# Four small edits in the gated layers: up products copied by ScalarE, squares on GpSimd, down products started from half of the features, two pieces more at the heads' norm

## The chip, the cores and the metric

The kernel runs on one core of a Trainium2 chip. A core has five engines that run their own instruction queues side by side: TensorE (PE, matrix products, with weight loads as PEld), VectorE (DVE), ScalarE (ACT), GpSimd (POOL), and SyncE (SP), which here issues DMAs. They share an on-chip memory (SBUF); PE writes its products into eight accumulator banks (PSUM), which DVE and ACT read. The metric is the device time of one launch in microseconds (us). All data is float32.

## The reference

Eight sequences of 512 tokens with 256 channels go through four residual layers, each `x = x + layer(...)`:

```python
x = x + attention(layernorm(x))       # 16 heads of 16 channels, 60% of the queries kept
x = x + routed_ffn(layernorm(x))
x = x + gated_layer(layernorm(x))     # linear attention over 8 steps, then swiglu, inside its own residuals
x = x + routed_ffn(layernorm(x))      # the same weights again
```

The change touches the last three. The routed layer picks 4 of 16 blocks of 64 hidden features for each token and computes `relu(x @ w1.T + b1)`, masked to the picked blocks, times `w2.T`. The gated layer:

```python
q, k, v, alpha, out_gate = ...        # projections of rmsnorm(x); alpha from a small gate net
S = alpha * S + k (outer) v;  o = q . S                # 16 heads of 16 channels, step by step
o = (o - mean(o)) / sqrt(var(o) + 1e-5)                # per head and token: "the heads' norm"
x = x + (o * out_gate) @ wo.T
x = x + (silu(n @ w_gate.T) * (n @ w_up.T)) @ w_down.T   # n = rmsnorm(x), 1024 features: "swiglu"
```

The eight sequences are the eight steps of the linear attention, so a slice of 128 positions can be worked through all layers alone.

## The kernel before, in words

The first 600 us are the attention of the first layer, with the scores of all heads. It is not touched. After it the tokens, which stay in SBUF as `xres` (128 positions x 8 sequences x 4 slices x 256 channels), are worked on in four slices `k` of 128 positions. For each slice there is an output projection of the attention, a routed layer, the linear attention `gla(k)`, `swiglu(k)` and a second routed layer.

Two kinds of work are woven into each other by `between(units, pieces, n)`: after each unit of a list it calls as many `next(pieces)` as keep `n` pieces spread evenly over the units. Units are the large matmuls; pieces are the stretches between two `yield`s of the generators `gla` and `route`, with most of DVE's, ACT's and POOL's work. The lists at the end of the program put, for example, the rest of `gla(2)` and the beginning of `gla(3)` beside `swiglu(1)`. The number of pieces of one `gla` is the constant `GLA`. The program's order is not the final one: a scheduler of the tile framework orders each engine's instructions again from its own estimates, and puts semaphore waits where data or buffers require it.

- **Units of a routed layer** (`routed_ffn`). For each half `g` of the sequences (512 columns) and each of 8 groups `f` of 128 hidden features: two matmuls 128x512 into a bank `h_ps` (L909), a ReLU with bias by ACT to SBUF (L917; in the last layer, every second by DVE, L915), and a multiplication by the mask on DVE (L918). Then the down product.
- **Units of swiglu**. For each `g` and `f` two units: gate, two matmuls into a bank `swi_ps` (L936) and a Silu by ACT into a tile `h` (L942); up, two matmuls into another bank and a product `h * up` on DVE, which reads the bank (L945). Then the down product.
- **The down product** (`down`, L880 to L899). For a pair `u` of sequences, two columns blocks `i` of one bank `y_ps`, each the sum over 8 features (L889, matmuls of 256 columns). A unit is four matmuls: half of the features of one block. When both blocks are full, DVE adds the bank to `xres` (L894). A half `g` has two pairs, so eight units.
- **Banks.** `h_ps` and `swi_ps` share three banks, `y_ps` has two, the pieces' products share three. Tiles `h` have eight buffers; other tiles of the pool `post` have two unless it is said.
- **Pieces of `gla`**: statistics, transposes into channels, projections (L1019) copied by ACT (L1024), then for each of two halves `m` of the heads a series of weighted sums: DVE computes products and sums (L1042, L1044, L1052) in a tile `pr`, POOL adds them up in `o` (L1069). `hold` (L876 to L878) makes POOL write one element of a tile that is about to be used from the newest swiglu or routed result, so that this series cannot run ahead of the units.
- **The heads' norm** ends the series of each `m`: `sq = o * o` by ACT (L1114), `o = o * gate` on POOL (L1115), the sum of the squares per head on DVE (L1116, `var`). After both `m`: square root by ACT (L1123), reciprocal on DVE (L1124), and `o = o * var` on DVE for each `m` (L1127). Then PE transposes `o` (L1136, `oT_ps`), ACT copies it (L1137) and the output projection `gla_y` follows (L1144).

Of the kernel before, what the change touches and what calls it, by code (L numbers as in the profile page):

```python
# [10 lines left out]
F32 = mybir.dt.float32  # L11
U8 = mybir.dt.uint8
AF = mybir.ActivationFunctionType
ALU = mybir.AluOpType
# [3 lines left out]
P = 128  # L18
NB = 8
L = 512  # L20
D = 256
# [17 lines left out]
def block_kernel(ctx: ExitStack, tc: tile.TileContext, t: dict, out: bass.AP):  # L39
    nc = tc.nc  # L40
# [58 lines left out]
    with ExitStack() as outer:  # L99
# [25 lines left out]
        with ExitStack() as inner:  # L125
# [413 lines left out]
            for n in range(len(steps) + LAG + 1):  # L539
# [47 lines left out]
                else:  # L587
                    if n >= LAG:
                        next(later, None)
                    b, i = divmod(n - LEAD, 16)  # L590
# [19 lines left out]
        w2 = load_chunked(wpool, "w2", t["f_w2T"], nc.sync)  # L610
        b2 = load_rows(wpool, "b2", t["L0_ffn_b2"], nc.sync)

        with tc.tile_pool(name="a_tail", bufs=2) as tail:
# [7 lines left out]
            for u in range(2):  # L621
                for m in range(NC2):
                    for i in range(4):
                        b = 2 * i + u
                        rows = bass.ts(i, 32)
                        ps = (bank if i % 2 else bank_m)(f"nrm_ps{b}")
# [42 lines left out]
    w_down = load_chunked(wpool, "w_down", t["b_w_downT"], nc.sync)  # L669
# [15 lines left out]
    post = ctx.enter_context(tc.tile_pool(name="post", bufs=2, side="right", reuse_waits="tile"))  # L685
    dram = ctx.enter_context(tc.tile_pool(name="dram", bufs=2, space=bass.MemoryType.DRAM))

    def bank_h(name):
        return ps_h.tile([P, 512], F32, tag="h", name=name)

    def bank_y(name):
        return ps_y.tile([P, 512], F32, tag="y", name=name)
# [7 lines left out]
    G4 = NB // 2  # L700
# [12 lines left out]
    def tokens(k, b, n=2):  # L713
        return xres[:, b : b + n, k, :]

    def pairs(y):
        return y.rearrange("p (b d) -> p b d", d=D)
# [159 lines left out]

        nc.gpsimd.tensor_copy(dst, newest[0])  # L878

    def down(h, w, k, g, u, last):  # L880

        b = G4 * g + 2 * u
        y = []

        def unit(i, half):
            if i == 0 and half == 0:
                y.append(bank_y("y_ps"))
            for f in range(NF // 2 * half, NF // 2 * (half + 1)):
                nc.tensor.matmul(  # L889
                    y[0][:, bass.ts(i, D)], h[f][:, bass.ts(2 * u + i, P)], w[:, f, :],  # L890
                    start=(f == 0), stop=(f == NF - 1),
                )
            if i == 1 and half == 1:
                nc.vector.tensor_tensor(tokens(k, b), tokens(k, b), pairs(y[0]), ALU.add)  # L894
                newest[0] = xres[0:1, b, k, 0:1]
                if last:
                    nc.sync.dma_start(out=out_v[:, b : b + 2, k, :], in_=tokens(k, b))

        return [functools.partial(unit, i, half) for i in range(2) for half in range(2)]  # L899

    def hidden():
        return post.tile([P, 512], F32, tag="h", name="h", bufs=8)
# [1 line left out]
    def routed_ffn(k, key, last):  # L904
        def unit(h, g, f):
            xT, mk = ready[key]
            ps = bank_h("h_ps")
            for c in range(NC2):
                nc.tensor.matmul(  # L909
                    ps, w1[:, c, bass.ts(f, P)], xT[g][:, c, :],  # L910
                    start=(c == 0), stop=(c == NC2 - 1),
                )
            hf = hidden()
            if last and f % 2:
                nc.vector.tensor_scalar(hf, ps, b1[:, f : f + 1], 0.0, ALU.add, ALU.max)  # L915
            else:
                nc.scalar.activation(hf, ps, AF.Relu, bias=b1[:, f : f + 1])  # L917
            nc.vector.tensor_tensor(hf, hf, mk[g][:, f, :], ALU.mult)  # L918
            h.append(hf)
            newest[0] = hf[0:1, 0:1]  # L920

        units = []
        for g in range(2):
            h = []
            units += [functools.partial(unit, h, g, f) for f in range(NF)]
            for u in range(2):
                units += down(h, w2, k, g, u, last)
        return units


    def swiglu(k):
        def unit(h, pg, g, f, w):
            zT = ready["z", k]
            ps = bank_h("swi_ps")
            for c in range(NC2):
                nc.tensor.matmul(  # L936
                    ps, w[:, c, bass.ts(f, P)], zT[g][:, c, :],
                    start=(c == 0), stop=(c == NC2 - 1),
                )
            if w is w_gate:  # L940
                hf = hidden()
                nc.scalar.activation(hf, ps, AF.Silu)  # L942
                h.append(hf)
            else:
                nc.vector.tensor_tensor(h[f], h[f], ps, ALU.mult)  # L945
                newest[0] = h[f][0:1, 0:1]

        units = []
        for g in range(2):
            h = []  # L950
            for f in range(NF):
                units += [functools.partial(unit, h, None, g, f, w) for w in (w_gate, w_up)]
            for u in range(2):
                units += down(h, w_down, k, g, u, False)
        return units


# [3 lines left out]
    def gla(k):  # L961
# [18 lines left out]
        ps = bank_l("gh_ps")  # L980
# [12 lines left out]
        for u in range(2):  # L993
            ps = [bank_l("al_ps") for g in range(2)]
# [6 lines left out]
            for g in range(2):  # L1001
                b = G4 * g + 2 * u
# [10 lines left out]
        o = [rest.tile([P, NB, P], F32, tag="o", name="o", bufs=2) for m in range(NC2)]  # L1013
# [48 lines left out]
        def heads(m):  # L1062


            def fours(x):
                return x.rearrange("p (u i) n -> p u i n", i=G4)

            def add(dst, src):
                nc.gpsimd.tensor_tensor(dst, dst, src, ALU.add)  # L1069

            made = rest.tile([P, 3, NB, P], F32, tag="made", name="made")
            gate = rest.tile([P, NB, P], F32, tag="gate", name="gate", bufs=2)
            for b in range(NB):
                project(made, gate, m, b)
                yield
            nc.scalar.activation(gate, gate, AF.Silu)
            key, q, v = (fours(made[:, i]) for i in range(3))
            a, out = fours(al[:, :, bass.ts(m, P)]), fours(o[m])

            def near(d):  # L1080
                n = G4 - d
                if d > 0:
                    nc.gpsimd.tensor_tensor(
                        key[:, :, 0:n, :], key[:, :, 0:n, :], a[:, :, d:, :], ALU.mult
                    )
                return q[:, :, d:, :], key[:, :, 0:n, :], v[:, :, 0:n, :]

            pr = weighed([near(0)])[0]
            nc.gpsimd.tensor_copy(out, pr)
            yield from pause(5)  # L1090
            pr = weighed([near(1)])[0]
            add(out[:, :, 1:, :], pr)
            yield from pause(4)
            for d in (2, 3):
                pr = weighed([near(d)])[0]
                add(out[:, :, d:, :], pr)
                yield from pause(4 - d // 3)
            nc.gpsimd.tensor_tensor(q[:, 1, 0, :], q[:, 1, 0, :], a[:, 1, 0, :], ALU.mult)
            nc.gpsimd.tensor_tensor(
                q[:, 1, 1:, :], q[:, 1, 1:, :], far[:, :, bass.ts(m, P)], ALU.mult  # L1100
            )
            every = [P, 2, G4, P]
            for s in (0, 2):
                pr = weighed([(
                    q[:, 1].unsqueeze(1).to_broadcast(every),
                    key[:, 0, s : s + 2, :].unsqueeze(2).to_broadcast(every),
                    v[:, 0, s : s + 2, :].unsqueeze(2).to_broadcast(every),
                )])[0]
                for i in range(2):
                    add(out[:, 1], pr[:, i])  # L1110
                yield from pause(5)
            sq = rest.tile([P, NB, P], F32, tag="pr", name="sq", bufs=2)
            hold(sq[0:1, 0, 0:1])
            nc.scalar.activation(sq, o[m], AF.Square)  # L1114
            nc.gpsimd.tensor_tensor(o[m], o[m], gate, ALU.mult)  # L1115
            nc.vector.tensor_reduce(var[:, m, :], heads_of(sq), AX.X, ALU.add)  # L1116
            yield
# [8 lines left out]
        for m in range(NC2):  # L1126
            nc.vector.tensor_tensor(  # L1127
                heads_of(o[m]), heads_of(o[m]),
                var[:, m, :].unsqueeze(2).to_broadcast([P, NB * P // DH, DH]), ALU.mult,
            )  # L1130
            yield
        for g in range(2):
            for m in range(NC2):
                ps = bank_l("oT_ps")
# [5 lines left out]
        for b in range(0, NB, 2):  # L1140
            y = bank_l("gla_y")
# [39 lines left out]
        ready["z", k] = zT  # L1181


    GLA = 92

    def chain(*gens):
        return itertools.chain(*gens)
# [18 lines left out]
    ps = bank_l("bog_ps")[:, 0:D]  # L1206
    nc.tensor.matmul(ps, ones, turned, start=True, stop=True)
    nc.vector.tensor_copy(bog.rearrange("p m n -> p (m n)"), ps)
    g = [gla(k) for k in range(4)]
    between(routed_ffn(0, (1, 0), False), route(1, (1, 1)), ROUTE)  # L1210
    between(routed_ffn(1, (1, 1), False), chain(route(2, (1, 2)), some(g[0], 44)), ROUTE + 44)
    between(routed_ffn(2, (1, 2), False), chain(g[0], some(g[1], 10)), GLA - 34)
    between(swiglu(0), chain(some(g[1], 66), route(3, (1, 3))), 66 + ROUTE)
    between(routed_ffn(3, (1, 3), False), chain(g[1], some(g[2], 34)), GLA - 42)
    between(swiglu(1), chain(g[2], some(g[3], 24)), GLA - 10)
    between(swiglu(2), chain(g[3], route(0, (2, 0))), GLA - 24 + ROUTE)
    between(swiglu(3), route(1, (2, 1)), ROUTE)
# [53 lines left out]
```

## Time and profile before

| | us |
|---|---|
| median of three runs | 1651.34 (1651.06 to 1651.93) |
| the profiled execution | 1653.55 |
| its span, first to last instruction | 1651.8 |
| PE busy / DVE / ACT / POOL | 1599.0 / 969.4 / 671.7 / 334.3 |

1.75 us of the profiled execution lie outside its span, and it is 2.2 us above the median of the three runs. By stretches of the span (bounds of the layers are approximate, as they overlap):

| stretch, us | what runs on PE | PE busy | DVE | ACT | POOL | granted clock |
|---|---|---|---|---|---|---|
| 0 to 600 | attention | 570.97 | 438.25 | 346.52 | 79.08 | 0.99 |
| 600 to 640 | output projections | 36.40 | 33.30 | 9.96 | 8.78 | 0.91 |
| 640 to 871 | routed layers 0, 1, 2, pieces of gla 0 and 1 | 223.85 | 132.19 | 87.72 | 67.99 | 0.98 |
| 871 to 1083 | swiglu 0, routed 3, gla 1 and 2 | 209.62 | 109.82 | 80.44 | 67.04 | 1.00 |
| 1083 to 1221 | swiglu 1, gla 2 and 3 | 133.80 | 68.81 | 50.15 | 47.83 | 0.98 |
| 1221 to 1335 | swiglu 2, gla 3 | 111.60 | 68.91 | 40.24 | 51.56 | 1.00 |
| 1335 to 1420 | swiglu 3 | 85.00 | 26.22 | 22.87 | 5.72 | 1.00 |
| 1420 to 1652 | the second routed layers | 227.78 | 91.93 | 33.83 | 6.26 | 1.00 |

In the profile's lines a group reads "line, engine, operation, output<-inputs, shape, count, busy us, mean ns of one, idle time before it and what ended it". A line of the waits reads "engine and operation that waited <- engine and operation that ended the wait: total us, times, longest us". A line of a timeline gives the start in the span, the duration of the run of like instructions, engine, line and tile, and in brackets the idle time before it with its releaser. The granted clock (PEclk) is the share of its full clock that PE was given.

### The profile page before, as it was taken

What the parts mean: (1) busy time and instruction counts of PE and PEld (TensorE: products, weight loads), DVE (VectorE), ACT (ScalarE), POOL (GpSimd) and SP (SyncE); (2) the same over time, 40 slices, a digit from 0 to 9 for tenths busy, and PEclk for the clock granted to TensorE, in tenths of its full rate; (3) what the DMA queues carried; (4) which work ended last, traced back from release to release, by engine and by line L of the source; (5) the groups of instructions that cost most, each with busy time, mean ns of one, the idle gap of its engine ahead of it and who ended that gap; (6) DMA issues with size and microseconds to landing.
All of it is one profiled execution on the core that took longest, in us unless ns stands there. A gap on an engine that the chain in (4) does not pass through costs nothing.

```text
span 1651.8 us, 19680 instructions
## 1 busy us (share of the span) xinstructions
PE 1599.0 (97%) x7378; PEld 820.1 (50%) x7378; DVE 969.4 (59%) x2015; ACT 671.7 (41%) x1208; POOL 334.3 (20%) x381
## 2 busy tenths in 40 slices
PE   7999999999999969999989999999999999999999
PEld 3323223333233237655564556555555556766666
DVE  6978776676667786447672666277355633344342
ACT  2366666665656814252346123622521352121010
POOL 3111111010000102114342442154223421000000
PEclk9999999999999979999999999999999999999999
DMA  3100000000000051010000001000000010011100
GB/s 109 40 2 3 2 2 3 2 2 3 2 3 3 2 165 26 3 37 13 1 1 0 1 1 27 0 0 1 0 1 1 0 26 1 20 33 35 43 26 26
DMA packets 24276, 27.58 MB, mean 17 GB/s; under 512 B 6229, under 2 KB 20725, under 8 KB 24181
## 3 DMA queue, kind: packets, MB, share of 16 engines
q1 hardware_dynamic: 23108, 24.75, 5.2%
q10 hardware_dynamic: 1072, 1.57, 0.3%
q8 instruction: 58, 0.95, 0.2%
q14 instruction: 38, 0.30, 0.1%
HBM read 21.20 MB, written 4.33 MB: 15 GB/s over the span
## 4 chain that ended last, share of the span: by engine, by line
PE 77%; DVE 14%; ACT 3%; POOL 3%; issue 1%; DMA 1%; SPq 0%; ACTq 0%; POOLq 0%; DVEq 0%
PE y_ps L889 16%; PE h_ps L909 11%; PE s L433 8%; PE s L422 8%; PE swi_ps L936 7%; PE proj_ps L1019 7%; PE av L442 7%; DVE pr L1052 2%; DVE pr L1042 2%; PE ao_ps L775 2%; PE q_ps L316 2%; PE gla_y L1144 2%; DVE mx L425 2%; PE v_ps L376 2%; PE k_ps L316 2%; POOL o L1069 1%
## 5 line engine op out<-in xcount | busy, mean ns | idle before, releaser
L425 DVE TENSOR_REDUCE mx<-s 128x1 f32<-128x512 f32 x512 | 329.0, 684 | 129.8 <-PE s L433 83.0
L437 ACT ACTIVATE e<-s 128x512 f32<-128x512 f32 x512 | 276.1, 599 | 179.0 <-PE s L433 103.5
L422 PE MATMUL s<-k,q 32*128 32x512 f32 x1024 | 298.9, 641 | 3.2 <-ACT k L367 2.5
L433 PE MATMUL s<-q,k 32*128 32x512 f32 x1024 | 294.3, 638 | 0.4 <-DVE mx L425 0.3
L889 PE MATMUL y_ps<-w,h 128*128 128x256 f32 x1024 | 232.9, 383 | 2.9 <-DVE h L918 2.9
L909 PE MATMUL h_ps<-xnT,w 128*128 128x512 f32 x512 | 229.8, 597 | 4.1 <-ACT h L917 4.1
L889 PEld LDWEIGHTS y_ps<-w,h 128*128 128x128 f32 x1024 | 194.1, 192 | 41.0 <-issue 10.8
L909 PEld LDWEIGHTS h_ps<-xnT,w 128*128 128x128 f32 x512 | 95.5, 191 | 113.8 <-issue 107.1
L442 PE MATMUL av<-e,va 128*32 128x512 f32 (+1 forms) x1120 | 141.9, 568 | 3.8 <-ACT e L437 2.4
L918 DVE TENSOR_TENSOR h<-h,mk 128x512 f32<-128x512 f32 x128 | 97.6, 774 | 78.9 <-ACT h L917 70.0
L917 ACT ACTIVATE h<-h_ps,b 128x512 f32<-128x512 f32 x96 | 65.6, 684 | 178.1 <-PE h_ps L909 178.0
L422 PEld LDWEIGHTS s<-k,q 32*128 32x128 f32 x1024 | 89.5, 184 | 86.0 <-DVE mx L425 56.1
L433 PEld LDWEIGHTS s<-q,k 32*128 32x128 f32 x1024 | 88.1, 183 | 80.8 <-ACT e L437 53.8
L894 DVE TENSOR_TENSOR xres<-xres,y_ps 128x512 f32<-128x512 f32 x48 | 32.8, 683 | 162.2 <-PE y_ps L889 125.0
L936 PE MATMUL swi_ps<-zT,w_gate 128*128 128x512 f32 x256 | 122.7, 599 | 4.8 <-DVE h L945 4.8
L936 PE MATMUL swi_ps<-zT,w_up 128*128 128x512 f32 x256 | 121.2, 594 | 0.0
L1019 PE MATMUL proj_ps<-q_w,rT 128*128 128x512 f32 x256 | 118.3, 601 | 0.0
L889 PE MATMUL y_ps<-w_down,h 128*128 128x256 f32 x512 | 116.8, 380 | 0.0
L889 PEld LDWEIGHTS y_ps<-w_down,h 128*128 128x128 f32 x512 | 95.7, 190 | 20.0 <-issue 8.5
L942 ACT ACTIVATE h<-swi_ps 128x512 f32<-128x512 f32 x64 | 38.2, 596 | 156.7 <-PE swi_ps L936 156.6
L1069 POOL TENSOR_TENSOR o<-o,pr 128x512 f32<-128x512 f32 (+2 forms) x56 | 80.9, 1444 | 58.9 <-DVE pr L1052 56.9
L797 POOL TENSOR_TENSOR xres<-xres,b 128x512 f32<-128x512 f32 x32 | 40.1, 1271 | 240.0 <-ACT row L737 217.7
(191 smaller groups left out, 1713.9 us busy)
## 6 DMA issues: line engine op xcount, KB each, us to landing
mk<-md SPq DMA_DIRECT2D x32, 256.0 KB
xres<-in_L_attn_a_x SPq DMA_DIRECT2D x8, 512.0 KB
out<-xres SPq DMA_DIRECT2D x16, 256.0 KB
q<-negT SPq DMA_DIRECT2D x128, 2.0 KB
neg<-negT SPq DMA_DIRECT2D x128, 2.0 KB
w<-in_f_w1T SPq DMA_DIRECT2D x1, 1024.0 KB
w<-in_f_w2T SPq DMA_DIRECT2D x1, 1024.0 KB
w_gate<-in_b_w_gateT SPq DMA_DIRECT2D x1, 1024.0 KB
```

What stands on the lines that cost most here:

```text
L316: nc.tensor.matmul(ps, w[:, c, bass.ts(m, P)], xnT[:, c, :], start=(c == 0), stop=(c == NC2 - 1),)
L422: nc.tensor.matmul(s, qs[e][rows, m, bass.ts(k, P)], ks[e][rows, m, :], start=True, stop=True)
L425: nc.vector.tensor_reduce(mx[:, b, 2 * e + m, r : r + 1], s, AX.X, ALU.max)
L433: nc.tensor.matmul(s, ks[e][rows, m, bass.ts(kt, P)], qs[e][rows, m, :], start=True, stop=True)
L437: nc.scalar.activation(ex, s, AF.Exp, scale=1.0 / DH**0.5)
L442: nc.tensor.matmul(av[32 * j : 32 * j + 32, queries], va[:, 8 * kt + 4 * m + j, e, :], es[j][:, queries], start=(kt == 0), stop=(kt == 3 a ...
L889: nc.tensor.matmul(y[0][:, bass.ts(i, D)], h[f][:, bass.ts(2 * u + i, P)], w[:, f, :], start=(f == 0), stop=(f == NF - 1),)
L909: nc.tensor.matmul(ps, w1[:, c, bass.ts(f, P)], xT[g][:, c, :], start=(c == 0), stop=(c == NC2 - 1),)
L918: nc.vector.tensor_tensor(hf, hf, mk[g][:, f, :], ALU.mult)
L936: nc.tensor.matmul(ps, w[:, c, bass.ts(f, P)], zT[g][:, c, :], start=(c == 0), stop=(c == NC2 - 1),)
L1019: nc.tensor.matmul(ps, rT[b // G4][:, c, bass.ts(b % G4, P)], q_w[:, c, m], start=(c == 0), stop=(c == NC2 - 1),)
L1069: nc.gpsimd.tensor_tensor(dst, dst, src, ALU.add)
```

## The change

Four edits.

(a) In swiglu the up product is copied from its bank to a new SBUF tile `up` by ACT, and DVE multiplies `h` by that tile, not by the bank. 64 such copies are new; the 64 products remain.

(b) `sq = o * o` is computed on POOL, not by ACT's Square. There are eight, each of 128x1024 elements.

(c) The eight units of a down product come in another order. Written as (pair `u`, block `i`, half of the features), it was (0,0,0), (0,0,1), (0,1,0), (0,1,1), (1,0,0) and so on; it is (0,0,0), (1,0,0), (0,0,1), (0,1,0), (0,1,1), (1,0,1), (1,1,0), (1,1,1). So the first two units, of the two banks, need only the first four groups of features. This holds in routed and gated layers.

(d) After each `o = o * var` two pieces are yielded, not one; `GLA` is 94 instead of 92, and the spreading of the later pieces shifts with it.

```diff
-    def down(h, w, k, g, u, last):
+    def down(h, w, k, g, last):
-        b = G4 * g + 2 * u
-        y = []
-        def unit(i, half):
+        y = {}
+        def unit(u, i, half):
+            b = G4 * g + 2 * u
             if i == 0 and half == 0:
-                y.append(bank_y("y_ps"))
+                y[u] = bank_y("y_ps")
             for f in range(NF // 2 * half, NF // 2 * (half + 1)):
                 nc.tensor.matmul(
-                    y[0][:, bass.ts(i, D)], h[f][:, bass.ts(2 * u + i, P)], w[:, f, :],
+                    y[u][:, bass.ts(i, D)], h[f][:, bass.ts(2 * u + i, P)], w[:, f, :],
...
-        return [functools.partial(unit, i, half) for i in range(2) for half in range(2)]
+        order = [(u, i, half) for u in range(2) for i in range(2) for half in range(2)]
+        order.insert(1, order.pop(G4))
+        return [functools.partial(unit, *n) for n in order]
...
-                nc.vector.tensor_tensor(h[f], h[f], ps, ALU.mult)
+                up = post.tile([P, 512], F32, tag="up", name="up")
+                nc.scalar.copy(up, ps)
+                nc.vector.tensor_tensor(h[f], h[f], up, ALU.mult)
...
-            nc.scalar.activation(sq, o[m], AF.Square)
+            nc.gpsimd.tensor_tensor(sq, o[m], o[m], ALU.mult)
             nc.gpsimd.tensor_tensor(o[m], o[m], gate, ALU.mult)
             nc.vector.tensor_reduce(var[:, m, :], heads_of(sq), AX.X, ALU.add)
...
                 var[:, m, :].unsqueeze(2).to_broadcast([P, NB * P // DH, DH]), ALU.mult,
             )
-            yield
+            yield from pause(2)
...
-    GLA = 92
+    GLA = 94
```

The scheduler's new orders follow from all four at once. Round the transposes `oT_ps` of the four slices PE's order becomes:

- slice 0, in routed layer 2: the first four transposes come after one matmul of the down product, where there were four;
- slice 1, in routed layer 3: the same order;
- slice 2, in swiglu 1: the first four transposes come after the fourth gate unit of the half, where the fourth up unit also stood before them;
- slice 3, in swiglu 2: after the seventh gate unit, where the seventh up unit and half of the eighth gate unit also stood before them; but four more matmuls of the down product stand between the last projection and them.

On DVE, in slices 2 and 3, the last products L1052 of the series stand ahead of a product `h * up` that stood ahead of them. SP's order is the same, and ACT has 49 table loads instead of 48, the one more in swiglu 3.

More of the change, by code (lines that the diff above doesn't have):

```diff
@@ L893, in unit @@
             if i == 1 and half == 1:
-                nc.vector.tensor_tensor(tokens(k, b), tokens(k, b), pairs(y[0]), ALU.add)
+                nc.vector.tensor_tensor(tokens(k, b), tokens(k, b), pairs(y[u]), ALU.add)
                 newest[0] = xres[0:1, b, k, 0:1]
@@ L925, in routed_ffn @@
             units += [functools.partial(unit, h, g, f) for f in range(NF)]
-            for u in range(2):
-                units += down(h, w2, k, g, u, last)
+            units += down(h, w2, k, g, last)
         return units
@@ L952, in swiglu @@
                 units += [functools.partial(unit, h, None, g, f, w) for w in (w_gate, w_up)]
-            for u in range(2):
-                units += down(h, w_down, k, g, u, False)
+            units += down(h, w_down, k, g, False)
         return units
```

## The prediction

> **What bounds the kernel now.** I read the share of each engine, then the whole PE's waits, then the timelines of PE, DVE, ACT and POOL round each wait, then the granted clock there. The engines:
>
> ```profile
> PE 1599.0 (97%) x7378; PEld 820.1 (50%) x7378; DVE 969.4 (59%) x2015; ACT 671.7 (41%) x1208; POOL 334.3 (20%) x381
> ```
>
> PE is the bound, and the matmuls are the same before and after. Only what PE waits for, and the clock it then gets, can move the time. The waits from 640 us on, where the change lies:
>
> ```profile
> PE swi_ps L936 <- DVE h L945: 4.8, 7, 1.2
> PE h_ps L909 <- ACT h L917: 4.1, 1, 4.1
> PE oT_ps L1136 <- DVE o L1127: 3.3, 2, 2.1
> PE y_ps L889 <- DVE h L918: 2.9, 3, 1.9
> ```
>
> They are small: 15.1 us, and no edit can win more than these and the slow clock behind them. The clock is the column PEclk of the table by windows (PE, PEld, DVE, ACT, POOL busy, then PEclk), here round the 4.09 us wait at 837.4 to 841.5:
>
> ```profile
> 832.00:838.00 6.00, 5.39 (x13) 2.09 (x11) 5.91 (x7) 0.69 (x1) 1.63 (x2) 1.00 0.00 0
> 838.00:842.00 4.00, 0.52 (x1) 0.50 (x2) 1.64 (x2) 2.21 (x3) 2.79 (x3) 0.79 0.00 0
> 842.00:846.00 4.00, 4.00 (x7) 1.78 (x6) 4.00 (x6) 2.95 (x5) 1.28 (x1) 0.50 0.00 0
> 846.00:850.00 4.00, 4.00 (x24) 3.48 (x23) 2.70 (x3) 0.84 (x2) 0.00 (x0) 0.86 0.02 6
> ```
>
> After the wait PE is granted half its clock to about 847. Against the usual pitch (0.43 us between records of 512 columns) that costs 3.3 us more, so this place costs 7.4. The 2.07 us wait at 1157.26 is followed by 0.72 (1156 to 1160) and costs 1.7 more, the 1.94 at 770.01 by 0.75 and 2.0 more; after the waits of 0.7 to 1.2 us the clock stays 1.00 (1302 to 1306).
>
> **The gains, by place.** PE waits on swi_ps because a bank holds an up product until DVE has multiplied it (0.68 us each), and DVE is busy with the heads. With (a) ScalarE copies it out. The nearest row for such a copy is the 128x512 one of L1137, 0.59 us: 64 x 0.59 = 38 us more on an engine busy 41%, beside PE. DVE's wait moves from bank to buffer `up` (2 of them, each reused 6.9 us later; at the waits DVE was some 4 us late), so no copy should block ScalarE's queue. The waits in swiglu 0 (0.72 + 0.72), swiglu 1 (1.16 + 0.31) and swiglu 2 (0.15) go: -3.1 (bounds -3.1 and 0, if DVE is later than now). The two others on swi_ps (0.66, 1.04) belong to the norms below.
>
> The down product of the second routed layer:
>
> ```profile
> 765.32 2.75 PE L889 MATMUL y_ps<-w,h 128*128 128x256 f32 x12
> 770.01 0.70 PE L889 MATMUL y_ps<-w,h 128*128 128x256 f32 x2 [1.94 <-DVE h L918]
> 771.20 4.98 PE L889 MATMUL y_ps<-w,h 128*128 128x256 f32 x14 [0.50 <-DVE h L918]
> ```
>
> Six matmuls of 0.43 us ran before h of feature 6 was there (769.96), then h of 7 (771.15). With (c) eight come that need only features 0 to 3, then 4 and 5, to 769.64: waits 0.32 and 0.76, 1.36 less than 2.44, and neither long enough for the clock: -1.4 - 2.0 = -3.4 (bounds -1.4, the clock falling anyway, and -4.4, no wait). The 0.46 at 1011.74 goes likewise. Gains: 3.1 + 3.4 + 0.5 = **-7.0**.
>
> **The losses: the four norms of the heads.** After POOL's last sum comes a chain, here of slice 2, in DVE's, ACT's and POOL's timelines and PE's end of it:
>
> ```profile
> 1152.70 1.22 DVE L1116 TENSOR_REDUCE var<-sq 128x64 f32<-128x1024 f32 x1 [2.92 <-ACT sq L1114]
> 1153.84 0.68 DVE L945 TENSOR_TENSOR h<-h,swi_ps 128x512 f32<-128x512 f32 x1
> 1154.90 0.95 DVE L1124 RECIPROCAL var<-var 128x128 f32<-128x128 f32 x1 [0.39 <-ACT var L1123]
> 1155.89 2.36 DVE L1127 TENSOR_TENSOR o<-o,var 128x1024 f32<-128x1024 f32 x2
> ...
> 1151.61 1.06 ACT L1114 ACTIVATE sq<-o 128x1024 f32<-128x1024 f32 x1 [5.39 <-POOL o L1069]
> ...
> 1148.66 2.92 POOL L1069 TENSOR_TENSOR o<-o,pr 128x512 f32<-128x512 f32 x2
> 1152.75 2.36 POOL L1115 TENSOR_TENSOR o<-o,gate 128x1024 f32<-128x1024 f32 x1 [1.17 <-ACT sq L1114]
> ...
> 1157.26 0.66 PE L1136 MATMUL oT_ps<-ident,o 128*128 128x128 f32 x4 [2.07 <-DVE o L1127]
> ```
>
> (b) puts the square on POOL. Its price there is not in this trace; L1115, a product of the same size on the same engine, takes 2.36, against 1.06 on ACT: +1.3 in a chain in which nothing overlaps. (It could be as quick as POOL's one-input 128x1024 copy, 1.15: +0.1.) Then o*gate starts behind the square on POOL's queue; that delays nothing, since L1115 ends before the variance is ready. SP's queue keeps its order. What is queued behind the reduce's wait on DVE is the mult of the next unit, and behind the variance's wait on ACT the next Silu and copy; PE stands at oT by then, and needs their banks only after it.
>
> How the rebuilt order stands beside this, since the scheduler places the transposes oT anew, pieces added or not:
> - Slice 0 (routed 2). PE's order was h x16, y x4, oT; it is h x16, y x1, oT. ACT no longer holds the ReLUs behind the square, so the 4.09 wait goes; PE does its last two units (1.72) and one y matmul (0.43) from 837.4 and stands at oT at 839.55. Chain: hold to 839.75, square to 842.1, reduce 843.3, mask mult 844.0, reciprocal 844.95, mult 845.55, o*var 846.75. Idle 7.2 and the same 3.3 of slow clock, 10.5 against 7.4: +3.1 (0 to +4).
> - Slice 1 (routed 3). PE's order is the same; transposes at 1016.3 rather than 1015.21: +1.1 (0 to +2).
> - Slice 2 (swiglu 1). DVE does its two L1052 ahead of a mult (-0.6); with the square +1.3, less 0.5 as ACT's Silu no longer stands before the table load: o*var 0.2 later. But one up unit (1.72) that stood before oT stands behind it, and PE comes 0.66 earlier: wait 2.07 + 0.66 + 1.72 + 0.2 = 4.65, against 2.73: +1.9, and slow clock, 0.8 over the 1.7 of now: +2.7 (+1 to +4.5).
> - Slice 3 (swiglu 2). The same chain, 0.2 later. From the last projection, three gate or up matmuls (0.86) fewer and four down matmuls (0.43) more lie before oT, so PE is 0.84 earlier: wait 1.21 + 1.04 + 0.84 + 0.2 = 3.3, against 2.25: +1.0. At 3.3 the clock falls, where it did not; between the 1.7 and 3.3 above: 2.2. +3.2 (+0.5 to +5).
>
> Losses: **+10.1**. The pause adds no work; what it moves is in these orders. One table load more (1.28) lies in swiglu 3, where PE waits for nothing: 0, or 1.3 if that cover were gone. The slow stretch at 1195 (1.8 us, no wait before it) may go or double.
>
> Sum: -7.0 + 10.1 = +3.1, on the profiled 1653.55: 1656.65. That run is 2.2 above the median 1651.34, so on the median's scale **1654.4**.
>
> A rule weighed: the Trainium skill, "TensorE: Matmul & The Clock Gate", Part 1, has the clock at half after an idle window of about 3.4 us. Row: 2.07 us of idling was enough at 1157. By the rule slice 3 (3.3) would stay fast and the sum be 2.2 less. I go by the row.
>
> And one that speaks against the change: "GPSIMD Engine Reference", Engine selection, calls GpSimd about twice as slow as VectorE for two inputs, and Key points has it contend with VectorE instructions with two SBUF inputs, which (a) makes of the mult. Rows for both are used here (2.36 against 1.06; next paragraph).
>
> **Rivals.**
> 1. Slower by more: the mults h*up now have two SBUF operands, as L918 has. L945 never took over 690 ns; L918 took 774 on average and 1.75 at 836.76, beside POOL's sums at 836.39. If at slices 1 to 3 two mults each lengthen by 1.07 in the chain, 3 x 2.1 = 6.4: 1660.8. Against: DVE is often idle there, waiting for POOL.
> 2. Faster: the chain starts earlier than I reckon, L us. DVE sat 1.56 and 2.03 us before its last L1042 waiting for POOL's hold (1144.57, 1291.70); new order may fill that. Each us gives about 4 (four places); it decides at L = 0.8. At L = 2: slices 0, 2, 3 give 6.0, slice 1 1.1, slice 3's clock 2.2: 3.1 - 9.3 = -6.2, 1645.1. Against: each link above is a measured duration.
> 3. No change: the waits on swi_ps move to y_ps, gains 3.9, but slice 0 costs nothing more (its price there is the least sure) and slice 3 keeps its clock: 10.1 - 3.1 - 2.2 = 4.8; +0.9, 1652.2.
>
> **How the numbers follow.** 0.2% (3.3 us) is about what a measurement of this kernel can tell from no change. Chances: forecast 0.45 (own range 1650 to 1660: slower 0.29, same 0.14, faster 0.02); rival 1 0.15 (slower); rival 2 0.28 (faster 0.26, same 0.02); rival 3 0.12 (same 0.06, both sides 0.03). Faster 0.31, same 0.22, slower 0.47. Range: from rival 2 with the clock at 770 kept at its best bound (1 us more), 1644, to rival 1 with slice 3 at +5 (1.8 more), 1662.6.
>
> **What would show it.** Right: no wait of swi_ps for an h in swiglu 0 and 1; waits at 770 under 1.2 with PEclk 1.00; sq on POOL of 2.3 to 2.4 us; the longest waits of PE at oT, some 7 (slice 0), 4.7 and 3.3 us, with PEclk near 0.5 behind. Wrong: o*var ending earlier than the times above, or mults h*up of over 0.8 us in the chain.

## The result and the profile after

The changed kernel takes 1671.66 us (median of 4 runs, 1670.51 to 1673.16) against 1651.49 (4 runs): the ratio is 1.0122, 95% interval 1.011 to 1.0135. It is 20 us slower; the forecast was 3 us slower, and its range ended at 1662.6.

The engines' shares and PE's waits of the changed kernel (its span is 1670.5 us, 18.7 more; L1130 is the product `o * var`, L1139 the transposes, L1028 the gate addition, L921 the mask, L949 the product `h * up`):

```profile
PE 1601.6 (96%) x7378; PEld 821.7 (49%) x7378; DVE 984.2 (59%) x2015; ACT 700.6 (42%) x1265; POOL 357.9 (21%) x389
...
PE oT_ps L1139 <- DVE o L1130: 20.6, 4, 8.8
...
PE proj_ps L1022 <- DVE gate L1028: 9.2, 4, 4.1
...
PE y_ps L890 <- DVE h L921: 1.8, 3, 1.1
...
PE y_ps L890 <- DVE h L949: 1.1, 1, 1.1
```

PE has the same 7378 matmuls; its busy time is 2.6 us longer, at a mean granted clock of 0.982 instead of 0.988. The waits on swi_ps (4.8) and on h_ps (4.1) are gone, as the prediction said. In their place PE stands 20.6 us at the transposes (3.3 before) and 9.2 us at the projections, a wait that the kernel before did not have.

To see where the time came from I compare when the same gate, up and h matmuls start in the two traces; the lengthening of a stretch is the difference at its end less that at its beginning. Beside the changed kernel stand four of the experiments below; bounds are times of the kernel before. The table compares single executions, and that of the kernel before took 2.2 us more than its median; the sums are 1.3 to 3.0 us below the differences of the medians that the experiments give.

| stretch, us | forecast | after | (a) alone | (b) alone | (a) + (b) | the same, product from the bank |
|---|---|---|---|---|---|---|
| to 640 | 0 | +0.3 | -0.2 | -0.5 | +0.2 | -1.7 |
| 640 to 785, the down product at 770 | -3.4 | -3.4 | 0.0 | 0.0 | -1.7 | 0.0 |
| 785 to 800, slice 0's projections | 0 | +2.3 | 0.0 | 0.0 | +0.6 | 0.0 |
| 800 to 880, slice 0's norm | +3.1 | +3.8 | -0.1 | +2.2 | +1.5 | +2.3 |
| 880 to 994, swiglu 0 | -1.4 | +0.2 | +1.5 | 0.0 | +1.5 | -1.7 |
| 994 to 1088, slice 1's norm | +0.6 | +2.2 | -0.1 | +1.7 | +3.3 | +3.3 |
| 1088 to 1145, slice 2's projections | -1.5 | +5.0 | 0.0 | 0.0 | +1.0 | +0.5 |
| 1145 to 1176, slice 2's norm | +2.7 | +2.8 | +1.3 | -1.2 | +3.9 | +2.4 |
| 1176 to 1222 | 0 | -2.0 | -0.1 | -1.7 | -0.2 | -1.9 |
| 1222 to 1282, slice 3's projections | -0.2 | +2.3 | +1.6 | 0.0 | +2.5 | +0.8 |
| 1282 to 1320, slice 3's norm | +3.2 | +5.0 | +1.1 | +1.0 | +4.7 | -0.5 |
| sum | +3.1 | +18.6 | +4.9 | +1.4 | +17.3 | +3.7 |

At four places the number came near the forecast: the down product at 770, and the norms of slices 0, 2 and, too small by 1.8, 3. Three stretches in which the projections of the second half of the heads run were forecast at -1.7 together and cost +9.6. PE's order changed there too, which the account of the change does not say: in slices 2 and 3 of the changed kernel some groups of four projection matmuls stand one unit earlier than before. With (a) and (b) alone they stand as before, the three stretches cost 4.1 (0.6 + 1.0 + 2.5), and the whole loss is the same. The stretch at 1176 held a slow clock before, with no wait ahead of it; in most of the later traces, also that with (c) alone, it is gone, so I do not put those 2 us down to the change.

### The profile page after: what moved, and what is told of

The parts are those of the page before. It is cut to its first block, busy times and chain, and to the rows that moved or that the text cites. A ratio compares the mean times of both kernels' runs of the same rounds, so it can differ in the third digit from the quotient of the medians.

```text
span 1670.5 us, 19750 instructions
## 1 busy us (share of the span) xinstructions
PE 1601.6 (96%) x7378; PEld 821.7 (49%) x7378; DVE 984.2 (59%) x2015; ACT 700.6 (42%) x1265; POOL 357.9 (21%) x389
## 4 chain that ended last, share of the span: by engine, by line
PE 72%; DVE 18%; POOL 5%; ACT 2%; issue 1%; DMA 1%; SPq 0%; ACTq 0%; POOLq 0%; DVEq 0%
PE y_ps L890 14%; PE h_ps L912 10%; PE s L433 8%; PE s L422 8%; PE av L442 7%; PE swi_ps L938 6%; PE proj_ps L1022 6%; DVE pr L1055 3%; POOL o L1072 3%; DVE pr L1045 3%; DVE w L1047 2%; PE ao_ps L775 2%; PE q_ps L316 2%; DVE mx L425 2%; PE gla_y L1147 2%; PE chT_ps L747 2%
## 5 line engine op out<-in xcount | busy, mean ns | idle before, releaser
L921 DVE TENSOR_TENSOR h<-h,mk 128x512 f32<-128x512 f32 x128 | 95.4, 758 | 77.7 <-ACT h L920 61.4
L1072 POOL TENSOR_TENSOR o<-o,pr 128x512 f32<-128x512 f32 (+2 forms) x56 | 87.0, 1554 | 61.4 <-DVE pr L1055 58.8
L949 DVE TENSOR_TENSOR h<-h,up 128x512 f32<-128x512 f32 x64 | 59.0, 924 | 64.6 <-ACT up L948 64.5
```

## What holds up DVE

Each slice works on the heads in two halves, one after the other. While the norm of the first half ends on POOL and DVE, PE already makes the projections of the second, and the banks of these projections are freed by DVE's gate additions (L1028), which stand in DVE's queue behind the reduce of the norm. The timelines of PE, DVE and POOL of the changed kernel in slice 2:

```profile
1111.88 3.78 PE L1022 MATMUL proj_ps<-q_w,rT 128*128 128x512 f32 x4 [4.10 <-DVE gate L1028]
...
1098.89 2.27 DVE L1045 TENSOR_TENSOR pr<-made 128x1024 f32<-128x1024 f32 x1
1101.09 1.75 DVE L949 TENSOR_TENSOR h<-h,up 128x512 f32<-128x512 f32 x1
...
1105.45 1.00 DVE L729 SCALAR_TENSOR_TENSOR ln_sh<-ln_mv,ln_rs 128x8 f32<-128x8 f32 x1
...
1106.97 1.23 DVE L971 TENSOR_TENSOR rr<-rr,ln_rs 128x8 f32<-128x8 f32 x1
...
1108.68 1.62 DVE L974 TENSOR_TENSOR rr<-rr,ln_rs 128x8 f32<-128x8 f32 x1
1110.33 0.17 DVE L729 SCALAR_TENSOR_TENSOR rr_sh<-ln_mv,rr 128x8 f32<-128x8 f32 x1
1110.42 1.21 DVE L1119 TENSOR_REDUCE var<-sq 128x64 f32<-128x1024 f32 x1
1111.55 0.48 DVE L1028 TENSOR_TENSOR gate<-proj_ps,bog 128x128 f32<-128x128 f32 x2
...
1098.82 3.47 POOL L1072 TENSOR_TENSOR o<-o,pr 128x512 f32<-128x512 f32 x2
1104.84 3.33 POOL L1072 TENSOR_TENSOR o<-o,pr 128x512 f32<-128x512 f32 x2 [2.55 <-DVE pr L1055]
1108.12 0.17 POOL L878 COPY sq<-h 1x1 f32<-1x1 f32 x1
1108.38 1.90 POOL L1117 TENSOR_TENSOR sq<-o 128x1024 f32<-128x1024 f32 x1
1110.35 2.36 POOL L1118 TENSOR_TENSOR o<-o,gate 128x1024 f32<-128x1024 f32 x1
```

DVE does not wait here for anything that its semaphores show: its instructions are long. The product `pr` takes 2.27 instead of 1.22, the product `h * up` 1.75 instead of 0.68, and three of 128x8, which take 0.17 elsewhere, 1.00, 1.23 and 1.62. Each of the five has two inputs in SBUF and runs beside an instruction of POOL; the three small ones end within 0.03 us of the end of a POOL sum or square. Together they are 5.5 us over. The reduce at 1110.42, with one input, runs beside POOL too and keeps its 1.21.

Not all of this is new. Here is the same place on DVE in the kernel before and, behind it, in the kernel with (a) and (b) whose product reads the bank (an experiment below; L947 is its product):

```profile
1092.52 2.29 DVE L1042 TENSOR_TENSOR pr<-made 128x1024 f32<-128x1024 f32 x1
...
1099.52 0.88 DVE L971 TENSOR_TENSOR rr<-rr,ln_rs 128x8 f32<-128x8 f32 x1
...
1101.61 1.22 DVE L1116 TENSOR_REDUCE var<-sq 128x64 f32<-128x1024 f32 x1 [1.02 <-ACT sq L1114]
```
```profile
1094.81 2.29 DVE L1044 TENSOR_TENSOR pr<-made 128x1024 f32<-128x1024 f32 x1
1097.02 0.67 DVE L947 TENSOR_TENSOR h<-h,swi_ps 128x512 f32<-128x512 f32 x1
...
1103.13 1.62 DVE L973 TENSOR_TENSOR rr<-rr,ln_rs 128x8 f32<-128x8 f32 x1
...
1104.87 1.21 DVE L1118 TENSOR_REDUCE var<-sq 128x64 f32<-128x1024 f32 x1
```

`pr` was as long before the change. From its start to the reduce it is 9.1 us before, 10.1 with the square on POOL and the product from the bank, and 11.5 in the changed kernel (in the kernel with (a) and (b) alone too). The 1.5 us from 10.1 to 11.5 are what the operand in SBUF costs at this place: 1.07 for `h * up`, and 0.4 for POOL's two sums, 3.33 instead of 2.93. The long small instructions are there with the product from the bank as well, and PE does not wait at the projections there.

The same in slice 3's norm, DVE and POOL:

```profile
1308.55 1.76 DVE L949 TENSOR_TENSOR h<-h,up 128x512 f32<-128x512 f32 x1
1313.56 1.22 DVE L1119 TENSOR_REDUCE var<-sq 128x64 f32<-128x1024 f32 x1 [3.25 <-POOL sq L1117]
1314.70 1.80 DVE L949 TENSOR_TENSOR h<-h,up 128x512 f32<-128x512 f32 x1
1316.42 0.94 DVE L1127 RECIPROCAL var<-var 128x128 f32<-128x128 f32 x1
1317.39 2.36 DVE L1130 TENSOR_TENSOR o<-o,var 128x1024 f32<-128x1024 f32 x2
...
1308.18 3.26 POOL L1072 TENSOR_TENSOR o<-o,pr 128x512 f32<-128x512 f32 x2 [3.38 <-DVE pr L1055]
1311.38 0.17 POOL L878 COPY sq<-h 1x1 f32<-1x1 f32 x1
1311.63 1.89 POOL L1117 TENSOR_TENSOR sq<-o 128x1024 f32<-128x1024 f32 x1
1313.60 2.35 POOL L1118 TENSOR_TENSOR o<-o,gate 128x1024 f32<-128x1024 f32 x1
```

POOL's product with the gate runs from 1313.60 to 1315.95. The product `h * up` comes at 1314.70 and ends at 1316.50, 0.55 after it. The square root on ACT was done at 1315.21, but the reciprocal stands behind `h * up` and starts at 1316.42. So the chain of the norm became longer by 0.8 us for the square (1.89 against ACT's 1.06) and again by 1.1 for a product that has nothing to do with it. The price shows in the group of the products, before and after:

```profile
L945 DVE TENSOR_TENSOR h<-h,swi_ps 128x512 f32<-128x512 f32 x64 | 43.5, 682 | 54.4 <-PE swi_ps L936 43.5 <-ACT h L942 4.8 <-PE chT_ps L747 3.4
```
```profile
L949 DVE TENSOR_TENSOR h<-h,up 128x512 f32<-128x512 f32 x64 | 59.0, 924 | 64.6 <-ACT up L948 64.5
```

The Trainium skill, "SBUF — State Buffer", section "SBUF: two separate sides", has a VectorE instruction with two SBUF inputs and a GpSimd instruction that reads SBUF lock each other out for a whole instruction, where the loser blocks fully. The row of 1314.70 (a product that ends 0.55 us after POOL's, having started 1.25 us before that end) agrees.

The slow clock at the new waits, from the windows of the changed kernel (after the window: its length, then PE, PEld, DVE, ACT and POOL busy, then PEclk):

```profile
1110.00:1114.00 4.00, 2.12 (x3) 1.09 (x4) 3.43 (x7) 0.00 (x0) 2.63 (x2) 0.56 0.00 0
1114.00:1118.00 4.00, 4.00 (x6) 1.54 (x6) 0.29 (x1) 0.48 (x1) 0.00 (x0) 0.59 0.00 0
...
1318.00:1322.00 4.00, 3.23 (x10) 2.12 (x11) 2.36 (x3) 0.69 (x2) 0.00 (x0) 0.50 0.00 0
```

Round the end of the 4.10 us wait at the projections, and for some 5 us behind it, PE has 0.56 to 0.59 of its clock, which adds about 2.8 to that wait (an estimate, from the starts of the next matmuls against their usual pitch of 0.43). The last row is behind the 6.17 us wait at slice 3's transposes.

## The experiments

The theories. A: the second SBUF operand of `h * up` costs, through POOL. B: the square on POOL costs, through the reduce and what stands behind it on DVE. C: the new order, from the pause and the scheduler, costs. Where a run's time is given as a difference, it is the difference of its median to that of the kernel before on the same chip.

**Each part taken back alone.**

```diff
-            nc.gpsimd.tensor_tensor(sq, o[m], o[m], ALU.mult)
+            nc.scalar.activation(sq, o[m], AF.Square)
```

> Undoes part (b) alone: the square is on ScalarE again, the rest is as after. Theory A (the product h*up from two SBUF operands is what costs: it and GpSimd's sums hold each other up, 0.92 us for 0.68 and 1.55 for 1.44, and so the whole series of the heads is late): most of the 20 us stays, 1665 or more; the products still take 0.9 us on average and the waits of PE for the gate additions stay. Theory B (the square on GpSimd is what costs: the reduce waits for it on DVE, and behind it in DVE's queue stand the gate additions that free PE's banks): the proj_ps waits (9.2 us) and some 4 us of slow clock go, 1655 to 1658. Theory C (the order of PE and the pause): no change within 3 us.

Measured: 1658.74 against 1651.57, ratio 1.0048 (1.0033 to 1.0063). Two thirds of the loss go, to just above the range that B gives. But three waits on proj_ps stay, of 1.42, 2.97 and 1.47 us, and the products still take 909 ns, as A says.

```diff
-                up = post.tile([P, 512], F32, tag="up", name="up")
-                nc.scalar.copy(up, ps)
-                nc.vector.tensor_tensor(h[f], h[f], up, ALU.mult)
+                nc.vector.tensor_tensor(h[f], h[f], ps, ALU.mult)
```

> Undoes part (a) alone: the product reads the bank again, no copies; square on GpSimd, new down order and pause stay. Theory A: products 0.68 us again, GpSimd's sums 1.45 us, proj_ps waits mostly gone though the square is still on GpSimd: 1653 to 1657, with the small swi_ps waits (about 4 us) back. Theory B: proj_ps waits stay, 1666 or more. Theory C: within 3 us of after.

Measured: 1658.35, ratio 1.0056 (1.0034 to 1.0078). Two thirds go here as well, to just above the range that A gives. Products 682 ns, POOL's sums 1506 (1554 after, 1444 before). From 1088 on nearly nothing of the loss is left (+0.6 us, after +13.2); what remains is slices 0 and 1, with a wait of 8.80 us at slice 0's transposes.

Neither theory alone explains that each of the two removals takes back two thirds of the same loss.

```diff
-            yield from pause(2)
+            yield
...
-    GLA = 94
+    GLA = 92
```

> Undoes part (d) alone: one piece after each o*var, GLA 92. Theories A and B: within 3 us of after, 1668 to 1674, since neither the square nor the products change. Theory C (the new place of the transposes, which came with the pause, makes PE stand at them for 20.6 us): oT_ps waits fall by half, 1660 or less.

Measured: 1670.19, ratio 1.0118 (1.0103 to 1.0133). The pause is not it, and theory C falls as far as it rests on the pause. With the old `GLA` the projections of slices 2 and 3 also stand where they stood before: slice 2's wait there falls from 4.10 to 2.37 us, but that at its transposes grows from 5.06 to 7.66.

**Parts alone.** First the order of the down units (the kernel before, with only `order.insert(1, order.pop(G4))`).

> The kernel before with part (c) alone, the order of the down units. PE's order round the transposes is that of before, so nothing but the y_ps waits should move: the waits at 770 fall from 2.44 to about 0.7 us, the slow clock behind them (2.0 us) goes and the 0.46 us at 1011 goes: 1647 to 1649, by all theories. If it is slower than 1651, the order of the down units has a cost that I have not seen.

Measured: 1650.3 against 1651.57, ratio 0.9992 (0.9981 to 1.0004): no clear difference. The waits at 770 fell to 0.22 and 0.50, as expected, and the stretch is 2.1 us shorter. But PE now came to slice 0's projections earlier, while DVE did not: there it waits 1.41 us, and 1.7 of the 2.1 us are given back. That wait was not expected. The granted clock behind it is 1.00 (788 to 808), so the expectation further below that speaks of a slower clock there has it wrong.

> Parts (c) and (d) without (a) and (b). If (a) and (b) carry the whole loss, 1648 to 1652, and the oT_ps waits at slices 2 and 3 under 3 us together. If the pause costs by itself, 1654 or more.

Measured: 1652.35, ratio 1.0005 (0.9996 to 1.0015). (c) and (d) together cost nothing that can be told; (a) and (b) carry the loss. PE waits 1.21 and 0.23 us for the transposes of slices 2 and 3, as expected of the two without the others.

```diff
+                up = post.tile([P, 512], F32, tag="up", name="up")
+                nc.scalar.copy(up, ps)
-                nc.vector.tensor_tensor(h[f], h[f], ps, ALU.mult)
+                nc.vector.tensor_tensor(h[f], h[f], up, ALU.mult)
```

> The kernel before with part (a) alone. If the second SBUF operand lengthens the series of the heads by itself, products of 0.9 us and GpSimd's sums of 1.55 us here too, projections of slice 2 waiting 2 to 3 us: 1655 to 1660. If (a) only costs together with the square on GpSimd: 1652 or less, the swi_ps waits (4.8 us) won.

Measured: 1657.77 against 1651.59, ratio 1.0038 (1.0024 to 1.0051). The products take 966 ns, POOL's sums 1527. The swi_ps waits for DVE go, and others come: 2.87 us at swiglu 0's down product for its last `h`, 1.74 at slice 3's projections, and on swi_ps itself 2.55 for ACT's copy at slice 2 and 2.63 for ACT's Silu at slice 3, since the square, which is still ACT's here and waits some 5.5 us for POOL, stands ahead of them in ACT's queue.

> The kernel before with part (b) alone. The square took 1.89 us on GpSimd against 1.06 on ScalarE: if the chain of the norm is all, 0.83 us later at each of four norms and the projections, with the slow clock 3 to 6 us: 1655 to 1658. The transposes' order in slice 3 is new here too (sixteen at once after the first matmul of the eighth gate unit), so up to 2 us may be its own.

Measured: 1655.95, ratio 1.0029 (1.0017 to 1.0041). The chain is 0.8 us later per norm; the cost that the table can place is at slices 0 and 1 (+2.2 and +1.7; the table's sum, +1.4, is 3.0 below the difference of the medians). At the projections nothing, so a reduce that waits 0.8 us longer is not enough to make PE wait there: the expected cost at that place was wrong.

**Both together, and what makes them more than their sum.**

> Parts (a) and (b) without (c) and (d). Alone they cost 6.2 and 4.4 us, the whole change 20.2; (c) and (d) together 0.2. If the rest, some 9 us, is what (a) and (b) do to each other (products and the square meet on GpSimd's and DVE's ways to SBUF, and DVE's waits add up in one queue): 1668 to 1673. If it needs the new down order or the pause: 1661 to 1664, the sum of both.

Measured: 1672.02 against 1651.7, ratio 1.0125 (1.0106 to 1.0143). (a) costs 6.2, (b) 4.4, both 20.3. So they make the whole loss by themselves, and 9.7 us of it only together (some 4 us either way, from the three intervals). Longer instructions are not what the pair has more: with (a) alone the products and POOL's sums are as long as with both, as this pair of lines shows beside those of (a) and (b) below.

```profile
L947 DVE TENSOR_TENSOR h<-h,up 128x512 f32<-128x512 f32 x64 | 61.6, 966 | 56.7 <-ACT up L946 56.6
...
L1071 POOL TENSOR_TENSOR o<-o,pr 128x512 f32<-128x512 f32 (+2 forms) x56 | 85.5, 1527 | 63.3 <-DVE pr L1054 61.0 <-DVE ln_rs L65 0.4 <-DVE ln_mv L63 0.4
```

What differs is where PE stands. With (a) alone it is held on swi_ps by ACT's queue in slices 2 and 3 (2.55 and 2.63 us) and waits only 0.51 and 1.01 us for the transposes. With both it is not held there, comes to the transposes early, and waits 6.42 and 4.79 us, for a chain that is also 0.9 us longer from POOL's last sum to `o * var`. How the 9.7 us add up from this, the slow clock behind the longer waits and the scheduler's place for the transposes, no run takes apart.

```diff
                 nc.scalar.copy(up, ps)
-                nc.vector.tensor_tensor(h[f], h[f], up, ALU.mult)
+                nc.vector.tensor_tensor(h[f], h[f], ps, ALU.mult)
```

> Parts (a) and (b), with ScalarE's copies kept but the product reading the bank. If what (a) and (b) do to each other comes through the product's second SBUF operand: 1655 to 1661, near the sum of (b) alone and a small cost of the copies, products 0.68 us. If the copies in ScalarE's queue and the place of the transposes are enough for it: within 3 us of the run above.

In this kernel, and in the next, the copies are made and read by nothing. Measured: 1657.84, ratio 1.0036 (1.0025 to 1.0048), 14.2 us less than with the operand in SBUF. Its products and POOL's sums, and those of the run above:

```profile
L947 DVE TENSOR_TENSOR h<-h,swi_ps 128x512 f32<-128x512 f32 x64 | 43.6, 683 | 57.3 <-ACT up L946 56.8
...
L1071 POOL TENSOR_TENSOR o<-o,pr 128x512 f32<-128x512 f32 (+2 forms) x56 | 80.9, 1444 | 62.2 <-DVE pr L1054 60.0 <-DVE ln_rs L65 0.4 <-DVE ln_mv L63 0.4
```
```profile
L947 DVE TENSOR_TENSOR h<-h,up 128x512 f32<-128x512 f32 x64 | 61.5, 964 | 56.6 <-ACT up L946 56.5
...
L1071 POOL TENSOR_TENSOR o<-o,pr 128x512 f32<-128x512 f32 (+2 forms) x56 | 85.5, 1527 | 63.3 <-DVE pr L1054 61.0 <-DVE ln_rs L65 0.4 <-DVE ln_mv L63 0.4
```

The products wait for ACT's copy in both. With the operand in the bank they are 683 ns again and POOL's sums are those of the kernel before, and the loss that needs both parts is gone: 6.1 us are left, 1.8 more than with (b) alone. The scheduler also sets the transposes of slice 2 otherwise in this kernel, after the first matmul of the last up unit, so that stretch (+2.4 against +3.9) is not told by the operand alone; the largest differences, slice 3 (-0.5 against +4.7) and swiglu 0 (-1.7 against +1.5), lie elsewhere.

> After, with ScalarE's 64 copies kept but the product reading the bank, as before; the copies are written and read by nobody, and ScalarE's queue, GpSimd's square, the down order and the pause are those of after. It tells the second SBUF operand of the product from the copy on ScalarE. If the operand costs (the product and GpSimd's instructions hold each other up): products 0.68 us on average, GpSimd's sums 1.45 to 1.50 us, and a time near that of the kernel without (a), 1656 to 1662, with swi_ps waits of some 4 us back. If the copies in ScalarE's queue, or the order that came with them, cost: 1668 or more.

The same in the changed kernel: 1661.32 against 1652.12, ratio 1.0061 (1.0046 to 1.0076), 9.2 us above the kernel before, where the changed kernel was 20.2 above. Products 683 ns, POOL's sums 1475. PE's proj_ps waits fall from 9.2 to 2.1 us; the swi_ps waits come back, larger than expected (10.3), since the bank is now kept until copy and product are both done.

**Is it the reduce that holds the gate additions?**

```diff
+            if late:
+                nc.gpsimd.tensor_copy(var[0:1, 0, 0:1], gate[0:1, NB - 1, 0:1])
+                nc.vector.tensor_reduce(var[:, 0, :], heads_of(late.pop()), AX.X, ALU.add)
```

This stands behind the eight projections of a half, and the reduce of the first half is taken from where it was.

> After, with the reduce of the squares of the first half of the heads made to wait, by one element that GpSimd copies from the last gate addition into its output, so that it stands behind the eight gate additions in DVE's queue and not ahead of them. PE's order is that of after. If the gate additions, and with them PE's banks, were held by the reduce that waits for GpSimd's square: proj_ps waits 9.2 -> under 2 us, the slow clock at two of them (about 3 us) goes: 1660 to 1664. If DVE is late there for what GpSimd does to its other instructions: proj_ps waits stay above 5 us and the time above 1667.

Measured: 1666.5, ratio 1.0086 (1.0069 to 1.0103). The waits on proj_ps fall from 9.2 to 4.1 us, between the two answers. Slice 3's 2.46 and swiglu 0's 0.60 go: there the reduce was what held the additions. Slice 0's falls from 2.05 to 1.29, and slice 2's from 4.10 only to 2.82: there DVE is late by long instructions ahead of the gate additions, in slice 2 those shown above, in slice 0 of this run two of 128x8:

```profile
787.85 1.66 DVE L971 TENSOR_TENSOR rr<-rr,ln_rs 128x8 f32<-128x8 f32 x1
...
789.66 2.29 DVE L729 SCALAR_TENSOR_TENSOR ln_sh<-ln_mv,ln_rs 128x8 f32<-128x8 f32 x1
```

> Part (c) alone, and the reduce of the first half of the heads behind the gate additions as in the run above. The down order alone made PE come to the projections of slice 0 some 2 us earlier, where it waited 1.41 us and ran at a slower clock. If the reduce is what holds the gate additions there, that wait goes: 1647 to 1649. If not: as the down order alone, 1650.

Measured: 1649.13 against 1652.12, ratio 0.9986 (0.9976 to 0.9995). It is faster than the kernel before, by about 2 to 3 us, but not for the reason expected: slice 0's wait at the projections is still 1.40 us. Ahead of the gate addition DVE now has a mask product of two SBUF inputs that takes 2.37 us beside POOL's product with the gate (1.81 behind the reduce, with the down order alone). What the reduce's place gave beyond the down order can't be told from these runs; the interval of the down order alone overlaps with this one's.

**Squares on a third engine.**

```diff
-            nc.scalar.activation(sq, o[m], AF.Square)
+            nc.vector.tensor_tensor(sq, o[m], o[m], ALU.mult)
```

> Part (c) alone, and the squares on DVE instead of ScalarE or GpSimd. ScalarE is then not held before the ReLUs of slice 0, so the wait on h_ps (4.2 us) goes, and the chain of the norm has one change of engine less: 1646 to 1649 if the square takes 1.2 us there. If DVE, which then stands still at the square, lets the gate additions or masks wait: 1651 or more.

Measured: 1649.78 against 1651.59, ratio 0.9993 (0.9984 to 1.0002): not told from no change. The square takes 1.23 us on DVE, and ACT is no longer held at slice 0; but PE then waits 5.75 us at the transposes in place of 4.2 at h_ps.

> The same with the reduce of the first half of the heads behind the gate additions. Against the run above: 0 to 2 us less at the projections of slice 0, where PE waits 1.4 us: 1645 to 1649; the square itself stays ahead of the gate additions.

Measured: 1651.86, ratio 1.0003 (0.9994 to 1.0011). No gain; the expectation was wrong.

## Why the prediction was wrong

- **Bound by PE, only its waits count.** Right: the same matmuls, 2.6 us more of busy time, all else is waits and clock.
- **The gains.** The -3.4 at the down product of 770 was met: its waits fell to 0.23 and 0.50, where 0.32 and 0.76 were reckoned. But 2.0 of it was a slow clock that does not always come (last section), so that the number is exact is luck; with (c) alone the same place gained 2.1. The waits on swi_ps went as said, but of the 3.1 us of swiglu 0 to 2 nothing was kept in sum: DVE, no earlier than before, made PE wait at the next thing that it must deliver. The second bound (0, "if DVE is later than now") was the one that came.
- **The price of the square.** 1.89 us, not the 2.36 of the nearest row: +0.83 rather than +1.3, within the bounds. The 1.06 set against it is ScalarE's; the comparison quoted there is with VectorE, on which the square took 1.23.
- **The first step that failed** is the term for (a). It enters the sum as a gain of 3.1 us alone; the forecast leaves DVE's and POOL's instructions as long as they were, and has the lengthening only in a rival. The runs show in its place: products of 924 ns for 682, 15.5 us over all 64, POOL's sums of 1554 for 1444, and 14.2 us of device time between the product from SBUF and from the bank with (a) and (b), about 11 in the changed kernel.
- **The second** is the sentence on what stands behind DVE's wait. It named the mult of the next unit, for the second half of the heads, and never looked at the first half. There the gate additions stand behind the reduce, and PE's projections behind these: 9.2 us of waits, and 9.6 us in the three stretches where -1.7 was reckoned, 11.3 of the 15.5 missed. Only a part is the reduce's: its move behind the additions took 5.1 of the 9.2 and some 5 us of time, (b) alone costs nothing at these places, and the product from the bank leaves 2.1 of the 9.2.
- **The norms** were right in where PE waits: PE stands at the transposes for 8.8, 5.1 and 6.2 us, where 7.2, 4.65 and 3.3 were reckoned. Slice 3 and slice 1 were too small by 1.8 and 1.6. In slice 3 the term "o*var 0.2 later" left out the 1.1 us by which `h * up` holds the reciprocal, and the lengthened instructions before. Slice 2's agreement is partly luck: its `h * up` took 1.80 and held the reciprocal in the same way, while the square was 0.47 cheaper than reckoned.
- **Rival 1** had the mechanism, two SBUF operands beside POOL. It was priced with the right delay (1.07 us a product), but only for two products in each of three norms, and at 0.15. Its sign, products of over 0.8 us in the chain, came. What was held against it, that DVE is often idle there, does not help where the product itself runs beside POOL (1308.55 and 1314.70 above). What it missed is that the delay also falls on the series ahead of the norms, whose lateness reaches PE through the transposes and the projections, and that (b) takes away PE's wait for ACT, behind which part of the lateness seems to hide with (a) alone. The two edits were priced each by itself and added: measured alone they cost 6.2 and 4.4, together 20.3.

## What to carry to other kernels

Moving an operand from PSUM to SBUF is not a neutral way to free a bank: where GpSimd works beside, a DVE product with two SBUF inputs pays up to the rest of GpSimd's instruction (0.68 us became 1.75 to 1.80 here), and so does all that is queued behind it. Price two edits together when both act on the same chain: here 6.2 and 4.4 us alone became 20.3. And for a wait that is added to a queue, list everything behind it at each place where it occurs, until something that PE needs; here the entries behind the reduce freed PE's banks.

## What was not expected of the hardware

- DVE instructions of 128x8 elements with two SBUF inputs, 0.17 us by themselves, took up to 1.62 us beside a POOL product in the changed kernel, and 2.29 in the run with the reduce moved. In the stretch of slice 2 DVE's one-input instructions took nothing more (reduce 1.21, reciprocals 0.19 and 0.20). But that is no rule: elsewhere one with a single tensor input and constants took 1.75, before the change as well as after, and ended 0.03 us after a POOL addition:

```profile
705.08 1.75 DVE L969 TENSOR_SCALAR rr<-rr 128x8 f32<-128x8 f32 x1
```

- POOL's product of a tile with itself, 128x1024, takes 1.89 us, that of two tiles 2.35.
- The length of a wait of about 2 us does not settle whether the slow clock follows: the same waits of 1.94 and 0.50 us at 770 were followed by 0.57 of the clock in the kernel before (772 to 776) and by 1.00 in the run with (a) and (b) alone, and the changed kernel's 2.05 us at 793 was followed by a full clock (windows below). So prices of 2 us for it at such waits are right at most on average. The Trainium skill, "TensorE: Matmul & The Clock Gate", Part 1, has the window run freely, so that the moment of a change depends on where in it the work falls. That would fit, but no run here shows it. The idle window of 3.4 us that it gives is longer than the waits that were enough here.

```profile
790.00:794.00 4.00, 1.95 (x5) 0.68 (x4) 3.90 (x12) 0.69 (x2) 2.34 (x1) 1.00 0.00 2
794.00:798.00 4.00, 4.00 (x10) 1.63 (x9) 2.30 (x7) 0.96 (x2) 0.00 (x0) 1.00 0.02 4
```
